# One transformer block on one core: issuing the score products of both head pairs of a slot in one interleaved order, and moving the full-array work between slots

## The chip, the cores and the metric

The kernel runs on 1 core of a Trainium2 chip, in one launch. The metric is the device time of that launch in microseconds (us), lower is better. TensorE (PE) multiplies matrices into PSUM, VectorE (DVE) and ScalarE (ACT) read PSUM, GpSimd (POOL) works on SBUF alone, and SyncE (SP) issues most of the DMA transfers.

## The reference

For 32 sequences of 512 tokens with 256 channels and 16 heads of 16 channels, all in float32:

```python
qk = x @ W_attn + b_attn                  # q and k; v is x itself
y  = causal_attn(q, k, v)                 # softmax(q k^T / 4) v, masked
e  = v[:, :, 1:] - y[:, :, :-1]
k2 = x[:, :-1] @ W_k2 + b_k2
y2 = causal_attn(q[:, :, 1:], k2, e)      # shifted by one, first row zero
x  = layernorm(x + proj(y) + proj(y2))
x  = layernorm(x + ffn(x))                # ffn: 8 experts, top 2
```

The tokens of the experts are those of the first sequence alone; every other sequence gets the two layer norms.

## The kernel before, in words

The 32 sequences have 4 **groups** of 4 heads each, 128 groups in all. `step(n)` works on several groups at once, as a pipeline: it projects for later groups, takes the largest scores of group n, the exponentials of group n-2 and of its second attention n-3, and the weighted values of n-2 and n-3.

A head has 16 channels but sits on 32 partitions, so the four heads of a group lie in the four row **quadrants** of the PE array. **Pair 0** is heads 0 and 1 (quadrants 0 and 1), **pair 1** is heads 2 and 3 (quadrants 2 and 3). Two kinds of work use quadrants:

- `maxima(n, u, pair)`: for one of five units u and one pair it fills a two-bank PSUM tile `sm` with four bf16 mask products (L206, `pick` times `hide`, widths 128, 96, 64, 32 or twice that) and then with the scores of queries with keys (L219); DVE then takes row maxima (L230) into `mx`.
- `scores(n, u, pair)`: it fills a PSUM tile `sc` with scores that lie the other way (L265, keys times `qm`); ACT takes exponentials into `pt` (L274), and POOL zeroes what is above the diagonal (L278).

Each float32 product of one head is two LDWEIGHTS and two MATMUL rows in the trace: two **passes**.

A step has five **slots**. In each slot s PE is given, in this order, `scores` of pair 1, `maxima` of pair 0, `scores` of pair 0, `maxima` of pair 1:

```python
for s in range(len(units)):
    for pair in range(2):
        scores(n - 2, s, 1 - pair)
        if ready(n):
            maxima(n, s, pair)
    for f in rest[s]:
        f()
```

What stands in `rest[s]` follows the slot and needs the whole array: `augment` (4 transposes `mt` of the maxima, L236; DVE adds q to give `qm`, L240), `normalize` (4 transposes `yt`, L304; DVE takes denominators, reciprocals and the scaled values, L308 to L324), `project` (`pj`, L169; ACT adds a bias into the staging tile `pk`, L173, and eight DMAs on SP's queue, L184, spread it over `q_t` or `kk_t`), `values` (`av`, 32 passes in column tiles, L289; ACT copies to `avs`, L297), once in four steps `turn` (`ys`, L355) and two halves of `attended` (`po`, L367, then layer norms on DVE and POOL), and in eight steps the experts (`hidden`, `down`).

PE's order is written out by hand (`manual_schedule`); the other engines are ordered by the tile framework. All PSUM tiles, of slots and of the rest, come from one pool of 4 buffers with two banks each, and the first product into a tile waits until the last reader of the buffer is done. `pk` has two one-buffer tags, `half0` and `half1`, which `hidden` uses too.

The order of a step before, with its full-array parts (which of them a step has depends on n mod 4):

| n mod 4 | order | PE time |
|---|---|---|
| 0 | s0, mt, yt, s1, po, s2, po, s3, av, s4, yt, pj, av | 24.91 us |
| 1 | s0, mt, yt, s1, pj, s2, s3, av, s4, yt, pj, av | 23.18 us |
| 2 | s0, mt, yt, s1, s2, s3, av, s4, yt, pj, av | 21.45 us |
| 3 | s0, mt, yt, s1, pj, s2, ys, s3, av, s4, yt, pj, av | 24.00 us |

Of the kernel before, what the change touches and what calls it, by code (L numbers as in the profile page):

```python
# [1 line left out]

# [6 lines left out]
F32 = mybir.dt.float32  # L9
BF16 = mybir.dt.bfloat16  # L10
I32 = mybir.dt.int32
AF = mybir.ActivationFunctionType
ALU = mybir.AluOpType
AX = mybir.AxisListType

P = 128
HD = 16
HS = 32
GH = 4
NH2 = 2  # L20
# [7 lines left out]
def block_kernel(  # L28
# [16 lines left out]
    nc = tc.nc  # L45
    B, T, C = x.shape
    NB = T // P
    NC = C // P
    NG = C // (GH * HD)
    E = w_gu.shape[0]  # L50
# [5 lines left out]
    const = ctx.enter_context(tc.tile_pool(name="const", bufs=1))  # L56
    seq = ctx.enter_context(tc.tile_pool(name="seq", bufs=2))
    grp = ctx.enter_context(tc.tile_pool(name="grp", bufs=3))
    work = ctx.enter_context(tc.tile_pool(name="work", bufs=2))
# [22 lines left out]
        )  # L82


    q_t = [const.tile([P, T], F32, name=f"q_t{i}") for i in range(4)]
    kk_t = [const.tile([P, 2, T], F32, name=f"kk_t{i}") for i in range(6)]
    wp_sb = const.tile([P, NC, C], F32, name="wp_sb")
    nc.scalar.dma_start(wp_sb, w_proj.rearrange("(c p) f -> p c f", p=P))
# [49 lines left out]
    seqs = {}  # L138
# [26 lines left out]
    def project(two, m):  # L165
        b, half = divmod(two, NG // 2)
        ps = bank2(f"pj{two}_{m}")
        for c in range(NC):
            nc.tensor.matmul(  # L169
                ps[:, 0], wq_sb[:, m, c, half * P : (half + 1) * P], seqs[b]["xT"][:, c], start=(c == 0), stop=(c == NC - 1)  # L170
            )
        pk = work.tile([P, T], F32, tag=f"half{(two + m) % 2}", name=f"pk{two}_{m}", bufs=1)
        nc.scalar.activation(pk, ps[:, 0], AF.Identity, bias=bp_qk[:, m, half : half + 1])  # L173
        for k in range(2):
            n = 2 * two + k
            d = groups.setdefault(n, {})
            if m == 0:
                t = d["q"] = q_t[n % len(q_t)]
            else:
                d["kk"] = kk_t[n % len(kk_t)]  # L180
                t = d["kk"][:, m - 1]
            for h in range(GH):
                r = (GH * k + h) * HD
                nc.sync.dma_start(t[HS * h : HS * h + HD], pk[r : r + HD])  # L184
# [10 lines left out]
    ]  # L195

    def maxima(n, u, pair):
        d = groups[n]
        parts, first, step, kinds = units[u]
        ps = bank2(f"sm{n}_{u}_{pair}")  # L200
        blocks = ps.rearrange("p h (k c) -> p h k c", c=P)
        heads = [(hh, slice(HS * (NH2 * pair + hh), HS * (NH2 * pair + hh + 1))) for hh in range(NH2)]

        for c in range(NB):
            for hh, rows in heads:
                nc.tensor.matmul(  # L206
                    blocks[:, hh, first::step, HS * c :],
                    pick[rows, c],
                    hide[rows, c, kinds[0] : kinds[1], HS * c :],
                    start=(c == 0),  # L210
                    stop=False,
                )
        for i, a, na, at in parts:
            nk = (i + 1) * P
            view = ps[:, :, at * P : at * P + na * nk].rearrange("p h (a k) -> p h a k", k=nk)
            order = [slice(i * P, nk), slice(0, i * P)] if i else [slice(0, P)]
            for keys in order:
                for hh, rows in heads:
                    nc.tensor.matmul(  # L219
                        view[:, hh, :, keys],  # L220
                        d["q"][rows, i * P : (i + 1) * P],
                        d["kk"][rows, a : a + na, keys],
                        start=False,
                        stop=(at == parts[-1][3] and keys == order[-1]),
                    )
        for i, a, na, at in parts:
            nk = (i + 1) * P
            view = ps[:, :, at * P : at * P + na * nk].rearrange("p h (a k) -> p h a k", k=nk)
            to = mx[n % 2][:, i, NH2 * pair : NH2 * (pair + 1), HD + a : HD + a + na]
            nc.vector.tensor_reduce(to, view, AX.X, ALU.max)  # L230

    def augment(n):
        d = groups[n]
        ps = bank2(f"mt{n}")
        for i in range(NB):
            nc.tensor.transpose(  # L236
                ps[:, 0, i * P : (i + 1) * P], mx[n % 2][:, i].rearrange("p h s -> p (h s)"), ident
            )
        d["qm"] = grp.tile([P, T], F32, tag="qm", name=f"qm{n}")
        nc.vector.tensor_add(d["qm"], ps[:, 0], d["q"])  # L240

# [9 lines left out]
    def scores(n, u, pair):  # L253
        parts = [p for p in banks[u] if 0 <= n - p[0] < n_all]
        if not parts:
            return
        ps = bank2(f"sc{n}_{u}_{pair}")
        pt = work.tile([P, NH2, T], F32, tag=f"pt{u}", name=f"pt{n}_{u}_{pair}")
        for a, j, at in parts:
            d = groups[n - a]  # L260
            nq = T - j * P
            d["pt", a, j, pair] = pt[:, :, at * P : at * P + nq]
            for hh in range(NH2):
                rows = slice(HS * (NH2 * pair + hh), HS * (NH2 * pair + hh + 1))
                nc.tensor.matmul(  # L265
                    ps[:, hh, at * P : at * P + nq],
                    d["kk"][rows, a, j * P : (j + 1) * P],
                    d["qm"][rows, j * P :],
                    start=True,
                    stop=True,  # L270
                )
        lo = parts[0][2] * P
        hi = parts[-1][2] * P + T - parts[-1][1] * P
        nc.scalar.activation(pt[:, :, lo:hi], ps[:, :, lo:hi], AF.Exp, scale=HD**-0.5)  # L274

        for a, j, at in parts:
            diag = pt[:, :, at * P : (at + 1) * P]
            nc.gpsimd.affine_select(  # L278
                diag, diag, pattern=[[0, NH2], [1, P]], compare_op=ALU.is_ge, fill=0.0, base=-a, channel_multiplier=-1
            )  # L280

    def values(n, a):
        b, g = divmod(n, NG)
        d = groups[n]
        vals = (v_pad, e_pad)[a]
        ps = bank2(f"av{n}_{a}")
        for j in range(NB):
            for h in range(GH):
                nc.tensor.matmul(  # L289
                    ps[HS * h : HS * (h + 1), 0, j * P :],  # L290
                    vals[:, j, g * GH + h, :],
                    d["pt", a, j, h // NH2][:, h % NH2],
                    start=(j == 0),
                    stop=(j == NB - 1),
                )
        avs = d["avs", a] = work.tile([P, T], F32, tag="avs", name=f"avs{n}_{a}")
        nc.scalar.copy(avs, ps[:, 0])  # L297

    def normalize(n, a):
# [3 lines left out]
        for i in range(NB):  # L303
            nc.tensor.transpose(ps[:, 0, i * P : (i + 1) * P], d["avs", a][:, i * P : (i + 1) * P], ident)  # L304
        got = ps[:, 0].rearrange("p (n h s) -> p n h s", h=GH, s=HS)
        den = small.tile([P, NB, GH], F32, tag="den", name=f"den{n}_{a}")

        nc.vector.tensor_scalar_max(den, got[:, :, :, HD], 1e-30)  # L308
        rden = small.tile([P, NB, GH], F32, tag="rden", name=f"rden{n}_{a}")
        nc.vector.reciprocal(rden, den)  # L310
        rb = rden.unsqueeze(3).to_broadcast([P, NB, GH, HD])
        cols = slice(g * GH * HD, (g + 1) * GH * HD)

# [68 lines left out]
    def twice_normed(b, half):  # L382
# [11 lines left out]
        for k in range(2):  # L394
            i = 2 * half + k
            nc.gpsimd.tensor_scalar(t[:, i], t[:, i], mv[:, k, 0:1], r[:, k : k + 1], ALU.subtract, ALU.mult)  # L396
        if half:
            nc.sync.dma_start(out[b].rearrange("(n p) c -> p n c", p=P), t)
            seqs.pop(b)


    moe = {}
# [90 lines left out]
    def step(n):  # L493
# [7 lines left out]
        if ready(n):  # L501
            prepare(n)
        if ready(n - 1):
            rest[0].append(lambda: augment(n - 1))
        if ready(n - 3):
            rest[0].append(lambda: normalize(n - 3, 0))
            rest[3].append(lambda: values(n - 3, 1))
            rest[4].append(lambda: normalize(n - 3, 1))
        two = n // 2 + 1
        if ready(2 * two):  # L510
            for m, s in [(0, 4)] if n % 2 == 0 else [(1, 1), (2, 4)]:
                rest[s].append(lambda m=m: project(two, m))
        if ready(n - 2):
            rest[4].append(lambda: values(n - 2, 0))
# [2 lines left out]
            rest[2].append(lambda: turn(b))  # L517
        b2, r2 = divmod(n - 5, NG)
        if r2 == NG - 1 and 0 <= b2 < B:
            rest[1].append(lambda: attended(b2, 0))  # L520
            rest[2].append(lambda: attended(b2, 1))
        e = n - first_expert
        if e == -1:
            rest[4] += [route, turn_tokens, lambda: load_expert(0)]
        if 0 <= e < E:
            if e + 1 < E:
                load_expert(e + 1)
            rest[1].append(lambda: hidden(e, 0))
            rest[2].append(lambda: hidden(e, 1))
            rest[4].append(lambda: down(e))  # L530
        if e == E:
            rest[4].append(lambda: second_norm(0, moe["acc"]))
        for s in range(len(units)):
            for pair in range(2):
                scores(n - 2, s, 1 - pair)
                if ready(n):
                    maxima(n, s, pair)
            for f in rest[s]:
                f()

# [1 line left out]
    load_next(0)  # L542
    for m in range(3):
        project(0, m)
    for n in range(max(n_all + 5, first_expert + E + 1)):
        step(n)


# [71 lines left out]
```

## Time and profile before

| | |
|---|---|
| median of 3 runs | 3235.0 us (3234.16 to 3240.43) |
| profiled execution, its own time | 3252.37 us |
| its span in the trace | 3250.7 us |
| PE busy | 3159.7 us (97%) |
| DVE / ACT / POOL busy | 1999.3 / 1668.7 / 1373.8 us |
| mean granted PE clock | 0.986 |
| four steps, n = 18 to 121 | 93.53 us, the same in 26 sequences within 0.01 us |

Busy time of PE is a union over quadrants that work at the same time, with modelled ends: 97% doesn't mean that all four quadrants are in use. The times of slots and parts below are from the first start of a part to the first start of the next in the timeline. A matmul's duration in the trace is longer than its stream[...].

### The profile page before, as it was taken

What the parts mean: (1) busy time and instruction counts of PE and PEld (TensorE: products, weight loads), DVE (VectorE), ACT (ScalarE), POOL (GpSimd) and SP (SyncE); (2) the same over time, 40 slices, a digit from 0 to 9 for tenths busy, and PEclk for the clock granted to TensorE, in tenths of its full rate; (3) what the DMA queues carried; (4) which work ended last, traced back from release to release, by engine and by line L of the source; (5) the groups of instructions that cost most, each with busy time, mean ns of one, the idle gap of its engine ahead of it and who ended that gap; (6) DMA issues with size and microseconds to landing.
All of it is one profiled execution on the core that took longest, in us unless ns stands there. A gap on an engine that the chain in (4) does not pass through costs nothing.

```text
span 3250.7 us, 98094 instructions
## 1 busy us (share of the span) xinstructions
PE 3159.7 (97%) x42312; PEld 2147.1 (66%) x42312; DVE 1999.3 (62%) x3120; ACT 1668.7 (51%) x1823; POOL 1373.8 (42%) x2847
## 2 busy tenths in 40 slices
PE   5999998999999999999999999999999999999997
PEld 4665555667666666666666666676767676676673
DVE  4664444566666666666666666666666666666662
ACT  2554344455555555555555555555555555555554
POOL 4333334344444344444444444444344444443444
PEclk8999999999999999999999999999999999999998
DMA  4111111111111111111111111111111111111110
GB/s 110 37 28 47 37 48 35 39 50 51 32 50 51 41 51 50 50 46 39 50 44 47 50 50 50 39 44 50 40 51 51 49 51 33 50 48 43 38 28 20
DMA packets 144241, 148.13 MB, mean 46 GB/s; under 512 B 40984, under 2 KB 108992, under 8 KB 143808
## 3 DMA queue, kind: packets, MB, share of 16 engines
q1 hardware_dynamic: 143296, 141.42, 16.0%
q8 instruction: 333, 5.46, 0.7%
q14 instruction: 100, 0.82, 0.1%
q10 hardware_dynamic: 416, 0.39, 0.0%
q0 software_dynamic: 96, 0.04, 0.0%
HBM read 74.63 MB, written 16.78 MB: 28 GB/s over the span
## 4 chain that ended last, share of the span: by engine, by line
PE 88%; POOL 5%; DVE 2%; ACT 2%; issue 1%; SPq 1%; DMA 1%; POOLq 0%; DVEq 0%; ACTq 0%
PE sm L219 28%; PE av L289 18%; PE sc L265 14%; PE pj L169 10%; PE sm L206 5%; PE yt L304 4%; POOL h L396 2%; PE mt L236 2%; PE po L367 2%; POOL pt L278 1%; PE gu L450 1%; PE ys L355 1%; PE dn L473 1%; ACT pt L274 1%; POOL r L393 1%
## 5 line engine op out<-in xcount | busy, mean ns | idle before, releaser
L230 DVE TENSOR_REDUCE mx<-sm 128x2 f32<-128x1024 f32 (+3 forms) x1792 | 1573.6, 916 | 965.2 <-PE sm L219 933.0
L274 ACT ACTIVATE pt<-sc 128x1024 f32<-128x1024 f32 (+1 forms) x1282 | 1297.3, 1023 | 683.7 <-PE sc L265 633.6
L219 PE MATMUL sm<-kk_t,q_t 32*128 32x128 f32 (+2 forms) x12288 | 1431.4, 360 | 13.2 <-DMA kk_t<-pk 13.2
L265 PE MATMUL sc<-qm,kk_t 32*128 32x256 f32 (+3 forms) x8192 | 1369.1, 444 | 1.4 <-DVE mx L230 1.2
L278 POOL TENSOR_SCALAR_AFFINE_SELECT pt<-pt 128x256 f32<-128x256 f32 x2048 | 793.1, 408 | 1256.2 <-ACT pt L274 1255.2
L219 PEld LDWEIGHTS sm<-kk_t,q_t 32*128 32x128 f32 x12288 | 920.7, 188 | 35.4 <-issue 8.5
L265 PEld LDWEIGHTS sc<-qm,kk_t 32*128 32x128 f32 x8192 | 711.1, 185 | 224.9 <-issue 134.6
L206 PE MATMUL sm<-hide,pick 32*128 32x128 bf16 (+5 forms) x10240 | 512.3, 217 | 3.8 <-ACT pt L274 3.4
L206 PEld LDWEIGHTS <-pick 32*128 32x128 bf16 x10240 | 368.8, 93 | 32.0 <-issue 12.3
L169 PE MATMUL pj<-xT,wq_sb 128*128 128x512 f32 x768 | 369.7, 604 | 19.8 <-DMA xT<-in_xT 19.8
L297 ACT COPY avs<-av 128x512 f32<-128x512 f32 x256 | 150.1, 586 | 453.3 <-PE av L289 453.3
L289 PE MATMUL av<-pt,e_pad 128*32 128x512 f32 (+3 forms) x4096 | 315.4, 449 | 24.3 <-ACT pt L274 17.2
L289 PE MATMUL av<-pt,v_pad 128*32 128x512 f32 (+3 forms) x4096 | 303.9, 437 | 4.8 <-POOL pt L278 4.8
L173 ACT ACTIVATE pk<-pj,bp_qk 128x512 f32<-128x512 f32 x192 | 132.0, 688 | 337.2 <-PE pj L169 316.4
L289 PEld LDWEIGHTS av<-pt,e_pad 128*32 128x32 f32 x4096 | 134.2, 112 | 243.2 <-issue 139.8
L289 PEld LDWEIGHTS av<-pt,v_pad 128*32 128x32 f32 x4096 | 120.0, 110 | 248.9 <-issue 115.0
L169 PEld LDWEIGHTS pj<-xT,wq_sb 128*128 128x128 f32 x768 | 131.5, 191 | 121.7 <-issue 93.9
L304 PE MATMUL yt<-ident,avs 128*128 128x128 f32 x1024 | 161.4, 280 | 3.8 <-DVE mx L230 2.9
L321 POOL TENSOR_TENSOR e_pad<-xs,y 128x256 f32<-128x256 f32 x128 | 93.4, 730 | 151.2 <-DVE y L320 151.1
L396 POOL TENSOR_SCALAR h<-h,mv,r 128x256 f32<-128x256 f32 x124 | 150.8, 1223 | 6.5
L367 PE MATMUL po<-wp_sb,ysT 128*128 128x256 f32 x512 | 131.4, 401 | 5.7 <-ACT pt L274 4.6
L325 POOL TENSOR_TENSOR y<-y,y 128x256 f32<-128x256 f32 x128 | 93.9, 734 | 90.6 <-DVE y L324 90.6
(76 smaller groups left out, 1405.5 us busy)
## 6 DMA issues: line engine op xcount, KB each, us to landing
kk_t<-pk SPq DMA_DIRECT2D x1024, 32.0 KB
xT<-in_xT SPq DMA_DIRECT2D x32, 512.0 KB
x<-in_x SPq DMA_DIRECT2D x32, 512.0 KB
q_t<-pk SPq DMA_DIRECT2D x512, 32.0 KB
xr<-in_x SPq DMA_DIRECT2D x32, 512.0 KB
out<-h SPq DMA_DIRECT2D x31, 512.0 KB
xs<-in_x SPq DMA_DIRECT2D x32, 384.0 KB
gu<-in_w_gu SPq DMA_DIRECT2D x8, 512.0 KB
```

What stands on the lines that cost most here:

```text
L169: nc.tensor.matmul(ps[:, 0], wq_sb[:, m, c, half * P : (half + 1) * P], seqs[b]["xT"][:, c], start=(c == 0), stop=(c == NC - 1))
L206: nc.tensor.matmul(blocks[:, hh, first::step, HS * c :], pick[rows, c], hide[rows, c, kinds[0] : kinds[1], HS * c :], start=(c == 0), stop ...
L219: nc.tensor.matmul(view[:, hh, :, keys], d["q"][rows, i * P : (i + 1) * P], d["kk"][rows, a : a + na, keys], start=False, stop=(at == part ...
L230: nc.vector.tensor_reduce(to, view, AX.X, ALU.max)
L265: nc.tensor.matmul(ps[:, hh, at * P : at * P + nq], d["kk"][rows, a, j * P : (j + 1) * P], d["qm"][rows, j * P :], start=True, stop=True,)
L274: nc.scalar.activation(pt[:, :, lo:hi], ps[:, :, lo:hi], AF.Exp, scale=HD**-0.5)
L278: nc.gpsimd.affine_select(diag, diag, pattern=[[0, NH2], [1, P]], compare_op=ALU.is_ge, fill=0.0, base=-a, channel_multiplier=-1)
L289: nc.tensor.matmul(ps[HS * h : HS * (h + 1), 0, j * P :], vals[:, j, g * GH + h, :], d["pt", a, j, h // NH2][:, h % NH2], start=(j == 0), ...
L297: nc.scalar.copy(avs, ps[:, 0])
L304: nc.tensor.transpose(ps[:, 0, i * P : (i + 1) * P], d["avs", a][:, i * P : (i + 1) * P], ident)
L367: nc.tensor.matmul(ps[:, 0, i * C : (i + 1) * C], s["ysT"][:, c, (2 * half + i) * P : (2 * half + i + 1) * P], wp_sb[:, c], start=(c == 0) ...
L396: nc.gpsimd.tensor_scalar(t[:, i], t[:, i], mv[:, k, 0:1], r[:, k : k + 1], ALU.subtract, ALU.mult)
```

## The change

Products of a slot are no longer issued as they are made. `maxima` and `scores` return a list of (cost, function) and a function that issues what follows on DVE, ACT and POOL; the new `slot` gives each pair its own stream (pair 0: `maxima`, then `scores`; pair 1: `scores`, then `maxima`), computes when each product would start if the pair's quadrants did nothing else, and issues all products sorted by the start of the **product before it** in its stream. The four masks come in the order 128, 32, 64, 96 instead of 128, 96, 64, 32.

The rest moves: `augment` from slot 0 to slot 3; the first `normalize` from slot 0 to slot 1; `project` from slot 4 to slot 1 (m=0) and slot 2 (m=2); the first `attended` and the first `hidden` from slot 1 to slot 0. Thus most steps have nothing between slots 0 and 1. The store of a result is issued one step later, in slot 1. `augment` adds q in two instructions, a copy on ACT and a sum on POOL, instead of one on DVE. `normalize` of the first attention drops the clamp of the denominator. `values` takes its key blocks in the order 0, 2, 1, 3 (first attention) and 0, 1, 3, 2 (second). There are 5 tiles `q_t` instead of 4, and the tag of `pk` is computed from `two * 3 + m` instead of `two + m`.

```diff
-        pk = work.tile([P, T], F32, tag=f"half{(two + m) % 2}", name=f"pk{two}_{m}", bufs=1)
+        pk = work.tile([P, T], F32, tag=f"half{(two * 3 + m) % 2}", name=f"pk{two}_{m}", bufs=1)
...
-        for c in range(NB):
-            for hh, rows in heads:
-                nc.tensor.matmul(
...
+        for c in (0, *range(NB - 1, 0, -1)):
+            work.append(((kinds[1] - kinds[0]) * (P - HS * c), partial(mask, c)))
...
+                work.append((4 * na * (keys.stop - keys.start), partial(score, view, i, a, na, keys, stop)))
+
+        def largest():
+            for view, to in views:
+                nc.vector.tensor_reduce(to, view, AX.X, ALU.max)
+
+        return work, largest
...
-        nc.vector.tensor_add(d["qm"], ps[:, 0], d["q"])
+        nc.scalar.copy(d["qm"], ps[:, 0])
+        nc.gpsimd.tensor_add(d["qm"], d["qm"], d["q"])
...
+    def slot(n, u):
+        streams = []
+        for pair in range(2):
+            sc = partial(scores, n - 2, u, pair)
+            mm = partial(maxima, n, u, pair) if 0 <= n < n_all else lambda: ([], lambda: None)
+            streams.append([mm, sc] if pair == 0 else [sc, mm])
+        todo = []
+        second = [(1, 0), (0, 0), (0, 1), (1, 1)]
+        started, done = [-1, -1], [0, 0]
+        for pair, k in second:
+            products, after = streams[pair][k]()
+            for m, (cost, emit) in enumerate(products):
+                last = m == len(products) - 1
+                todo.append((started[pair], len(todo), pair, emit, after if last else None))
+                started[pair], done[pair] = done[pair], done[pair] + cost
+        for _, _, pair, emit, after in sorted(todo, key=lambda t: t[:2]):
+            for hh in range(NH2):
+                h = NH2 * pair + hh
+                emit(hh, slice(HS * h, HS * (h + 1)))
+            if after:
+                after()
...
-        for j in range(NB):
+        order = [0, 2, 1, 3] if a == 0 else [0, 1, 3, 2]
+        for j in order:
...
-        nc.vector.tensor_scalar_max(den, got[:, :, :, HD], 1e-30)
+        if a:
+            den = small.tile([P, NB, GH], F32, tag="den", name=f"den{n}")
+            nc.vector.tensor_scalar_max(den, sums, 1e-30)
...
-            rest[0].append(lambda: augment(n - 1))
+            rest[3].append(lambda: augment(n - 1))
         if ready(n - 3):
-            rest[0].append(lambda: normalize(n - 3, 0))
+            rest[1].append(lambda: normalize(n - 3, 0))
...
-            for m, s in [(0, 4)] if n % 2 == 0 else [(1, 1), (2, 4)]:
+            for m, s in [(0, 1)] if n % 2 == 0 else [(1, 1), (2, 2)]:
...
-            rest[1].append(lambda: attended(b2, 0))
+            rest[0].append(lambda: attended(b2, 0))
...
+            rest[1].append(lambda: store(b3))
...
-            rest[1].append(lambda: hidden(e, 0))
+            rest[0].append(lambda: hidden(e, 0))
...
-            for pair in range(2):
-                scores(n - 2, s, 1 - pair)
-                if ready(n):
-                    maxima(n, s, pair)
+            slot(n, s)
```

## The prediction

> **What bounds the kernel now.** First the shares of busy time and the chain that ended last, from the page.
>
> ```profile
> PE 3159.7 (97%) x42312; PEld 2147.1 (66%) x42312; DVE 1999.3 (62%) x3120; ACT 1668.7 (51%) x1823; POOL 1373.8 (42%) x2847
> ...
> PE 88%; POOL 5%; DVE 2%; ACT 2%; issue 1%; SPq 1%; DMA 1%; POOLq 0%; DVEq 0%; ACTq 0%
> ```
>
> PE carries the time. But 97% is a union over four quadrants, so the question is how full they are. PE's timeline of one slot 0 tells:
>
> ```profile
> 1501.72 0.48 PE L265 MATMUL sc<-qm,kk_t 32*128 32x256 f32 x2
> 1501.75 0.32 PE L206 MATMUL sm<-hide,pick 32*128 32x128 bf16 x8
> ...
> 1502.26 0.60 PE L265 MATMUL sc<-qm,kk_t 32*128 32x256 f32 x4
> 1502.55 0.48 PE L219 MATMUL sm<-kk_t,q_t 32*128 32x384 f32 x2
> 1502.87 0.38 PE L265 MATMUL sc<-qm,kk_t 32*128 32x256 f32 x2
> 1502.89 0.32 PE L206 MATMUL sm<-hide,pick 32*128 32x128 bf16 x8
> ```
>
> Pair 1's last `sc` pass starts at 1502.48 and streams 0.21 us, so its quadrants are free at 1502.69. Its masks start only at 1502.89, just after pair 0's `sc` began at 1502.87. Before that, pair 0's quadrants had four later passes issued and waiting (two products of two). In slot 3, with only two such passes waiting, pair 1 was not held (masks at 1515.67, where its `sc` ended). I read: about four passes of one quadrant can stand issued, and a fifth blocks everything behind it, whatever its quadrant. Slots 0, 2 and 4 lose 0.2 to 0.3 us to this.
>
> Slot 1 loses more, to something else:
>
> ```profile
> 1503.08 2.36 DVE L230 TENSOR_REDUCE mx<-sm 128x2 f32<-128x1024 f32 x2 [3.62 <-PE sm L219]
> 1505.36 0.68 DVE L240 TENSOR_TENSOR qm<-mt,q_t 128x512 f32<-128x512 f32 x1
> 1505.49 0.37 PE L206 MATMUL sm<-hide,pick 32*128 32x256 bf16 x4
> 1506.44 0.42 DVE L320 TENSOR_TENSOR y<-yt,rden 128x256 f32<-128x256 f32 x1
> 1506.92 0.42 PE L206 MATMUL sm<-hide,pick 32*128 32x256 bf16 x6
> ```
>
> Pair 0's masks (1505.49) wait for the second reduction of slot 0, which ended at 1505.44, pair 1's (1506.92) for the PSUM tile of `yt`, which DVE released at 1506.86; its quadrants were free at 1506.08. The short gap `mt`, `yt` (1.02 us) put DVE's work in the way. Slots standing alone take 2.37, 3.14, 2.60, 2.40 and 2.63 us to the next part; without a pause between them slots 2 and 3 take 5.21, slots 1 to 3 8.54.
>
> Last, what a semaphore wait does to matmuls behind it, from the timeline near the end:
>
> ```profile
> 3215.17 1.07 PE L289 MATMUL av<-pt,v_pad 128*32 128x512 f32 x8
> ...
> 3215.84 1.68 POOL L278 TENSOR_SCALAR_AFFINE_SELECT pt<-pt 128x256 f32<-128x256 f32 x4 [2.01 <-ACT pt L274]
> 3217.22 1.50 PE L289 MATMUL av<-pt,v_pad 128*32 128x384 f32 x24 [0.98 <-POOL pt L278]
> ```
>
> The second key block waits for POOL until 3217.22. The third (256 wide, 3217.89) had its data long before and still came after it. So a waiting product holds all later ones.
>
> **What the skill says.** The Trainium skill, "Perfetto Trace Analysis", section "Tensor Engine Instruction (MATMUL, LD_WEIGHTS)", has PE's instructions wait for semaphores in a queue and then move to an execution FIFO with limited reorder; the 3217 lines agree with the first part. "TensorE: Matmul & The Clock Gate", section "The mechanism", says that matmuls keep program order and only LDWEIGHTS is pulled ahead. The trace differs: masks issued after both `sc` products started at 1501.75, before the first product's second pass (1502.04). Across quadrants order isn't kept; the measurement decides.
>
> **The change, part by part.** Times of one profiled execution, sums per four steps (93.54 us before).
>
> *Slots alone.* With each pair free to run, pair 1 of slot 0 takes 0.11 (start) + 0.85 (`sc`, 2048 columns in all passes) + 0.16 (masks) + 0.92 (two products; 0.85 streaming, the rest the first weight load, seen as a first pass of 351 ns instead of 270) = 2.04 us, and 0.1 to drain: 2.14. The new order never puts more than two products (four passes) of a quadrant in the queue, so I let it reach that. Slot 3 likewise 2.14 (now 2.40); slots 1, 2 and 4 have masks twice as wide, 0.28: 2.24, 2.23 and 2.24 (now 3.14, 2.60, 2.63). The new mask order shows at most 0.05 per slot, and it is in these.
>
> *Slots without a pause (joints).* These are slots 0 and 1 in three steps of four, slots 2 and 3 where n mod 4 = 2. By the built program's order and PSUM buffers, a joint's second slot (1 or 3) issues `sc` of pair 1, two masks of pair 0, and then **the first mask of pair 1**, whose buffer is freed by the second exponential of the slot before. Exponentials take 1.02 us; they start 1.26 and 2.31 into slot 0 (1527.89 after a slot that began at 1526.63), so it is free at 3.39. Pair 0's own buffer is free at 2.62 (first reduction 1.34 to 2.57). Hence pair 0 stands from 2.7 to 3.39, behind a wait that isn't its own. Then its masks 0.14, products 0.90, `sc` 0.85: 5.28; pair 1, interleaved, ends at 5.26. With the drain 5.38, against 2.37 + 3.14 now. Slots 2 and 3 joined come to 5.40 by the same working, no better than now.
>
> *Rest.* `mt` before `av` hides behind nothing new, 0.49 as before. `yt` 0.49, `pj` 1.81 (1.91 ahead of a slot), `av` 2.29, `po` 1.92 and `ys` 1.02 keep their time. What is late next: after a joint `pj` waits for the first reduction of slot 1 (0.11); `yt` after slot 4 for an exponential (0.1); where n mod 4 = 0, `pj` stands 0.45 behind the layer norm on DVE, `po` 0.2 and 0.1 behind exponentials, and `av` 0.32 behind DVE; where it is 3, slot 3 is held by the copy of `ysT` (2.50 instead of 2.14).
>
> | n mod 4 | sum after | before |
> |---|---|---|
> | 0 | 2.35+1.92+2.24+0.10+0.49+0.45+1.91+2.23+0.11+1.92+2.14+0.21+0.50+0.32+2.29+2.24+0.11+0.49+2.29 = 24.31 | 24.91 |
> | 1 | 5.38+0.49+0.11+1.91+2.23+0.12+1.91+2.24+0.11+0.50+2.29+2.24+0.10+0.49+2.29 = 22.41 | 23.18 |
> | 2 | 5.38+0.49+0.12+1.91+5.40+0.49+0.05+2.29+2.24+0.10+0.49+2.29 = 21.25 | 21.45 |
> | 3 | 5.38+0.49+0.12+1.91+2.23+0.11+1.81+1.02+2.50+0.50+2.29+2.24+0.10+0.49+2.29 = 23.48 | 24.00 |
>
> Together 91.45: 2.09 us less per four steps.
>
> *Other engines.* DVE loses 128 sums of 680 ns and 128 clamps of 164; ACT gains 128 copies (586, as `avs`), POOL 128 sums (about 1.3 us, as `sig` and `hid` of 128x512). All have idle time (POOL 42% busy); `qm` is needed a step later, after `av`, slot 4, `yt` and `av` (7 us) against 0.6 + 1.3 and POOL's queue of selects (0.41 each). I cost it at nothing; without that cover it would be up to 1.9 per step. The DMAs of `project` keep their count and go out earlier; the result's store no longer stands on SP ahead of them. The tag of `pk` doesn't change: 3·two + m and two + m have the same parity. The fifth `q_t` costs one ACT activation at the start (0.71).
>
> *Sum.* 118 steps without experts are 29.5 times 2.09: 62 us. The end: `values` finds ready blocks while it waits, about -2; the start +0.7. The eight steps with experts (34.8 to 49.9 us each) have their own waits (table loads, `pk` and `hf` sharing tiles, a DVE instruction idle for 4.1 us); nothing before shows the new order, so I take 0 and bound it by 2 us a step, -16 to +16. In all -63: 3252.4 becomes 3189; the median shown lies 17.4 below the profiled execution, so 3172.
>
> **Rivals.** *No holding.* If pair 0 went on past pair 1's waiting mask, joints of slots 0 and 1 would end 0.64 sooner, the other 0.55, as its own buffers are free then: 4.56 instead of 2.09 per four steps, 3100. For it: quadrants do overtake each other. Against: 3217.
>
> *Weights late (slower).* A product now enters the queue only when the one before it starts. If that leaves its first weight load exposed as it is after a mask (351 - 270 = 81 ns), on each of some 20 products of a pair per step rather than on 5, it costs 15 x 0.081 = 1.2 us a step, 4.9 per four, net +2.8: 29.5 times that, 3318. It decides from 35 ns per product on. Against it: within a product the second pass follows with no gap[...].
>
> *DVE and ACT take it back.* In joints the reductions (1.22 us, two a slot) and exponentials set the pace, more than I count; at 0.5 us a joint the gain is gone: 3235.
>
> **How the numbers follow.** The forecast case gets 0.55, no holding 0.2, late weights 0.15, taken back 0.1. The forecast's own range is 3172 with 16 for the experts and 0.05 us for each of 20 slots in four steps (30 us): 3130 to 3215. The range goes down to no holding, 3095, and up to 3225; late weights stay outside. About 0.2%, 6.5 us, can be told from no change. Of the taken-back case half ends faster, half the same: faster 0.8, same 0.05, slower 0.15.
>
> **What would show it.** Right: slots 0, 2 and 4 alone 0.2 to 0.4 shorter; pair 1's masks starting where its `sc` ends; slots 0 and 1 joined at 5.4 with pair 0 standing 0.7 inside slot 1; four steps near 91.5. Wrong: joints near 4.8 (no holding), or first passes of 350 ns on most products (late weights); expert steps longer by over 2 us.

## The result and the profile after

On chips where both kernels ran in turns, the median fell from 3247.3 us (20 runs) to 3234.2 us (20 runs): the ratio is 0.9961, with a 95% interval of 0.9948 to 0.9973. The change makes the kernel faster by 0.4%, and not by the 2% forecast. The profiled execution of the changed kernel has a span of 3233.4 us against 3250.7 before.

The first lines to compare are again the shares of busy time and the shares of the chain that ended last (the chain of work followed back from the last instruction), from the page of the kernel after:

```profile
PE 3057.4 (95%) x42312; PEld 1947.3 (60%) x42312; DVE 1867.3 (58%) x2864; ACT 1734.0 (54%) x1956; POOL 1538.0 (48%) x2975
...
PE 61%; ACT 7%; POOL 7%; DVE 4%; issue 3%; SPq 0%; ACTq 0%; POOLq 0%; DMA 0%; DVEq 0%
```

PE has 102 us less busy time, and the span is only 17 us shorter. PE is busy for less of the time. The shares of the chain add up to 82% here, since it could be followed back only to 573 us; of what it covers PE has three quarters, where it had 88%. What PE saved inside the slots came back as waits. The page's costliest groups name one of them:

```profile
L335 PE MATMUL av<-pt,v_pad 128*32 128x512 f32 (+3 forms) x4096 | 309.5, 437 | 41.6 <-POOL pt L294 40.7
```

The last two numbers are idle time of PE just before these matmuls: 41.6 us, 40.7 of it until POOL had zeroed a tile `pt`. By step, with each step counted from the start of slot 0 (means over 24 sequences):

| n mod 4 | before | forecast | after |
|---|---|---|---|
| 0 | 24.91 | 24.31 | 25.72 |
| 1 | 23.18 | 22.41 | 22.52 |
| 2 | 21.45 | 21.25 | 21.45 |
| 3 | 24.00 | 23.48 | 23.41 |
| sum | 93.53 | 91.45 | 93.10 |

Three of the four steps come out within 0.2 us of the forecast. The step with n mod 4 = 0 is 1.4 us over it and is longer than before. (With n mod 4 = 2 that still means no gain at all, where 0.2 was forecast.) POOL's timeline of the last part of one such step (it starts at 1494.26) shows why. The columns are start, duration, engine, line and operation, and in brackets the idle time before it and what ended it:

```profile
1510.80 2.43 POOL L445 TENSOR_SCALAR h<-h,mv,r 128x256 f32<-128x256 f32 x2
1513.19 0.42 POOL L294 TENSOR_SCALAR_AFFINE_SELECT pt<-pt 128x256 f32<-128x256 f32 x1
1514.26 2.36 POOL L399 TENSOR_TENSOR xr<-xr,bp 128x1024 f32<-128x1024 f32 x1 [0.65 <-DMA xr<-in_x]
1516.56 0.42 POOL L294 TENSOR_SCALAR_AFFINE_SELECT pt<-pt 128x256 f32<-128x256 f32 x1
1516.93 1.30 POOL L253 TENSOR_TENSOR qm<-qm,q_t 128x512 f32<-128x512 f32 x1
1518.17 1.51 POOL L294 TENSOR_SCALAR_AFFINE_SELECT pt<-pt 128x256 f32<-128x256 f32 x4
```

The same stretch in PE's timeline:

```profile
1515.49 0.66 PE L350 MATMUL yt<-ident,avs 128*128 128x128 f32 x4
1517.04 1.50 PE L335 MATMUL av<-pt,v_pad 128*32 128x512 f32 x16 [0.89 <-POOL pt L294]
1519.37 1.07 PE L335 MATMUL av<-pt,v_pad 128*32 128x384 f32 x16 [0.83 <-POOL pt L294]
```

POOL has a second half of a layer norm, the sum `xr<-xr,bp` with a wait for its load, and the new sum `qm` to do, and the six selects that `av` needs stand between and behind them. `av` starts 1.55 us after `yt` instead of the 0.59 of the other steps, and stops once more in the middle, for 0.83. Over all steps with n mod 4 = 0, `av` starts 0.85 to 1.55 after `yt`, 1.17 on average, and takes 3.33 instead of 2.29. Before, the same work of POOL, in a step that starts at 1501.72:

```profile
1518.24 2.43 POOL L396 TENSOR_SCALAR h<-h,mv,r 128x256 f32<-128x256 f32 x2
1520.62 0.41 POOL L278 TENSOR_SCALAR_AFFINE_SELECT pt<-pt 128x256 f32<-128x256 f32 x1
1521.00 2.36 POOL L350 TENSOR_TENSOR xr<-xr,bp 128x1024 f32<-128x1024 f32 x1
1523.31 1.84 POOL L278 TENSOR_SCALAR_AFFINE_SELECT pt<-pt 128x256 f32<-128x256 f32 x5
```

Here the selects follow `xr` at once, without `qm`, and `pj` (1.81 us of PE) stood between `yt` and `av`, which began at 1524.34 without a wait. Counted from the start of the step, POOL's layer norm ends at the same place in both kernels (18.95 and 18.97), but its last select ends at 23.4 before and at 25.4 now.

The wait for the load of `xr` comes from the change too. SP's queue in the same step of the kernel after:

```profile
1504.44 5.80 SPq L185 DMA_DIRECT2D q_t<-pk  x8
1510.33 0.54 SPq L398 DMA_DIRECT2D xr<-in_x  x1
```

The old `xr` was read for the last time by the sum `h<-po,xr`, which ended at 1508.60. The load of the next one stands on SP behind the eight DMAs of `project`, which now run after slot 1, and went out 1.7 us later (1.25 on average over such steps). In the kernel before nothing stood there, and it went out 0.03 us after that sum. In the changed kernel POOL waits 0 to 0.66 us for this load, 0.29 on average, and in each of 26 such steps `av` starts 0.85 to 0.90 us plus that wait after `yt`.

Inside the joints the hold that the forecast described is there. PE's timeline in a joint of slots 0 and 1 that starts at 1542.89:

```profile
1545.59 0.31 PE L208 MATMUL sm<-hide,pick 32*128 32x256 bf16 x4
...
1546.25 0.32 PE L208 MATMUL sm<-hide,pick 32*128 32x256 bf16 x6
1546.41 0.63 PE L221 MATMUL sm<-kk_t,q_t 32*128 32x128 f32 x6
```

Pair 0 starts two masks (four rows, two heads) from 1545.59 on and then nothing until 1546.25, right after ACT's second exponential ended and pair 1's first mask got its buffer; the two exponentials in ACT's timeline end at 1546.20:

```profile
1544.15 2.05 ACT L290 ACTIVATE pt<-sc 128x1024 f32<-128x1024 f32 x2 [0.48 <-PE sc L275]
```

The joint takes 5.28 us.

### The profile page after: what moved, and what is told of

Its sections match the earlier page's. It is cut to its first block, busy times and chain, and to the rows that moved or that the text cites. A ratio compares the mean times of both kernels' runs of the same rounds, so it can differ in the third digit from the quotient of the medians.

```text
span 3233.4 us, 97999 instructions
## 1 busy us (share of the span) xinstructions
PE 3057.4 (95%) x42312; PEld 1947.3 (60%) x42312; DVE 1867.3 (58%) x2864; ACT 1734.0 (54%) x1956; POOL 1538.0 (48%) x2975
## 4 chain that ended last, share of the span: by engine, by line
PE 61%; ACT 7%; POOL 7%; DVE 4%; issue 3%; SPq 0%; ACTq 0%; POOLq 0%; DMA 0%; DVEq 0%
PE sm L221 13%; PE av L335 13%; PE sc L275 12%; PE pj L170 10%; ACT pt L290 7%; PE po L416 4%; PE yt L350 3%; PE sm L208 3%; POOL h L445 2%; POOL pt L294 2%; PE mt L248 2%; DVE st L438 1%; DVE h L423 1%; POOL qm L253 1%; DVE mx L240 1%
## 5 line engine op out<-in xcount | busy, mean ns | idle before, releaser
L240 DVE TENSOR_REDUCE mx<-sm 128x2 f32<-128x1024 f32 (+3 forms) x1792 | 1541.1, 914 | 1092.1 <-PE sm L221 1083.0
L275 PE MATMUL sc<-qm,kk_t 32*128 32x256 f32 (+3 forms) x8192 | 1384.3, 448 | 26.2 <-ACT pt L290 7.8
L221 PE MATMUL sm<-kk_t,q_t 32*128 32x128 f32 (+2 forms) x12288 | 1286.0, 351 | 12.8 <-DMA kk_t<-pk 12.8
L221 PEld LDWEIGHTS sm<-kk_t,q_t 32*128 32x128 f32 x12288 | 909.7, 187 | 29.3 <-DMA kk_t<-pk 13.6
L208 PE MATMUL sm<-hide,pick 32*128 32x128 bf16 (+5 forms) x10240 | 541.1, 216 | 8.5 <-DVE mx L240 7.8
L170 PE MATMUL pj<-xT,wq_sb 128*128 128x512 f32 x768 | 386.2, 627 | 29.5 <-DMA xT<-in_xT 19.5
L208 PEld LDWEIGHTS <-pick 32*128 32x128 bf16 x10240 | 351.4, 92 | 84.2 <-issue 67.4
L335 PE MATMUL av<-pt,v_pad 128*32 128x512 f32 (+3 forms) x4096 | 309.5, 437 | 41.6 <-POOL pt L294 40.7
L335 PEld LDWEIGHTS av<-pt,e_pad 128*32 128x32 f32 x4096 | 124.3, 111 | 160.8 <-issue 126.3
L253 POOL TENSOR_TENSOR qm<-qm,q_t 128x512 f32<-128x512 f32 x128 | 163.9, 1281 | 16.9 <-ACT qm L252 9.6
L350 PEld LDWEIGHTS yt<-ident,avs 128*128 128x128 f32 x1024 | 108.5, 142 | 65.9 <-ACT pt L290 50.5
```

Of the source, the lines that this page charges most:

```text
L170: nc.tensor.matmul(ps[:, 0], wq_sb[:, m, c, half * P : (half + 1) * P], seqs[b]["xT"][:, c], start=(c == 0), stop=(c == NC - 1))
L208: nc.tensor.matmul(blocks[:, hh, first::step, HS * c :], pick[rows, c], hide[rows, c, kinds[0] : kinds[1], HS * c :], start=(c == 0), stop ...
L221: nc.tensor.matmul(view[:, hh, :, keys], d["q"][rows, i * P : (i + 1) * P], d["kk"][rows, a : a + na, keys], start=False, stop=stop,)
L253: nc.gpsimd.tensor_add(d["qm"], d["qm"], d["q"])
L275: nc.tensor.matmul(ps[:, hh, at * P : at * P + T - j * P], d["kk"][rows, a, j * P : (j + 1) * P], d["qm"][rows, j * P :], start=True, stop ...
L335: nc.tensor.matmul(ps[HS * h : HS * (h + 1), 0, j * P :], vals[:, j, g * GH + h, :], d["pt", a, j, h // NH2][:, h % NH2], start=(j == orde ...
```

## The experiments

The theory: the parts on PE went nearly as forecast, and POOL's queue at the end of steps with n mod 4 = 0 took back three quarters of the gain. Three parts of the change meet there: `qm` summed on POOL, `project` moved out of slot 4, and slots that end earlier. The rivals: the hold in joints is the whole loss; or the merged order gives nothing at all and the moves are what counts.

**qm back to one DVE sum.**

```diff
-        nc.scalar.copy(d["qm"], ps[:, 0])
-        nc.gpsimd.tensor_add(d["qm"], d["qm"], d["q"])
+        nc.vector.tensor_add(d["qm"], ps[:, 0], d["q"])
```

> The changed kernel with one part undone: qm is again one DVE sum from PSUM, so POOL has no qm sum (1.28 us each). Theory POOL: in the step with n mod 4 = 0 POOL works without a break for 10 us (layer norm, xr, selects, qm), and values waits 1.04 us inside for the selects behind qm; that wait goes, four steps drop from 93.1 to about 92.1, the whole by some 31 us (1.3 to 1.4% below the kernel before, which the changed kernel is by 0.4%). The 0 to 1 us that yt and the start of av lose in this step stays, since it stands behind xr and not behind qm. Theory PE order: the gain was lost in the slots; then nothing moves by more than 0.2%.

Measured: 3209.4 us, 0.9888 of before (0.9872 to 0.9904); four steps 92.2. `av` never waits inside any more: it takes 2.29 us, and the step with n mod 4 = 0 falls to 24.8. A wait ahead of `av` remains in these steps, with `yt` to `av` 0.85 to 1.90: the sum `xr` and the wait for its load are still in front of the selects. The theory holds, with a part left over; the whole is 1.1% below before, where 1.3 to 1.4% was expected.

**The sum xr moved to DVE.**

```diff
-        nc.gpsimd.tensor_add(s["xr"], s["xr"], bp2.unsqueeze(1).to_broadcast([P, NB, C]))
+        nc.vector.tensor_add(s["xr"], s["xr"], bp2.unsqueeze(1).to_broadcast([P, NB, C]))
```

> The changed kernel with the sum of xr and the bias (2.36 us once in four steps) on DVE instead of POOL; qm stays on ACT and POOL. Theory POOL: both waits of the step with n mod 4 = 0 go (about 0.6 us on average ahead of av, 1.04 us inside), less up to 0.3 for DVE's extra work: four steps 91.5 to 91.8, the whole 1.7 to 1.9% below the kernel before. Theory PE order: within 0.2% of the changed kernel.

Measured: 3302.4 us, 1.0183 of before (1.0159 to 1.0206). A miss, and an instructive one. DVE's timeline:

```profile
1541.68 1.95 DVE L399 TENSOR_TENSOR xr<-xr,bp 128x1024 f32<-128x1024 f32 x1 [3.60 <-DMA xr<-in_x]
1543.55 2.41 DVE L240 TENSOR_REDUCE mx<-sm 128x2 f32<-128x1024 f32 x3
```

The load of `xr` goes out when the sum `h<-po,xr` has read the old tile and SP's queue is past the DMAs of `project`, and the framework puts the sum of `xr` early in DVE's order. DVE stands 3.60 us for the load, and the reductions that release PSUM stand behind it; over the whole run it is 96.9 us in 31 such waits. POOL also stood for this load, for 0.65 us, because other work kept it busy until then. The Trainium skill, "Perfetto Trace Analysis", section "Tensor Engine Instruction (MATMUL, LD_WEIGHTS)", calls DVE, ACT and GpSimd strictly first in, first out; these lines agree. Slot 4 of these steps takes 5.42 us on average instead of 2.34. Moving the sum was no test of the theory, since it added a wait of its own, so the sum was left out instead.

**The sum xr left out.** The kernel then lacks the bias of the projection in its result.

```diff
-        nc.gpsimd.tensor_add(s["xr"], s["xr"], bp2.unsqueeze(1).to_broadcast([P, NB, C]))
```

> After, with POOL's sum xr<-xr,bp left out (the output lacks the bias of the projection). Theory (POOL's queue in the last part of steps n mod 4 = 0 is what av waits for; the sum takes 2.36 and 0.65 of waiting for its load there): three us less in that queue, the waits of yt and av gone, the step at 24.3 as forecast, 29 times 1.4 = 41 us less than after: 0.983 to 0.985 of before. Rival (av waits for ACT's exponentials, and POOL only shows as the last in line): 0.993 or more.

Measured: 3180.8 us, 0.9803 of before (0.9781 to 0.9824), a little more gain than expected. The step with n mod 4 = 0 takes 24.10 us and four steps 91.5; the forecast had 24.31 and 91.45. POOL's timeline at the same place, then PE's:

```profile
1502.90 0.77 POOL L294 TENSOR_SCALAR_AFFINE_SELECT pt<-pt 128x256 f32<-128x256 f32 x2
1503.65 1.27 POOL L253 TENSOR_TENSOR qm<-qm,q_t 128x512 f32<-128x512 f32 x1
1505.23 0.77 POOL L294 TENSOR_SCALAR_AFFINE_SELECT pt<-pt 128x256 f32<-128x256 f32 x2 [0.32 <-ACT pt L290]
```

```profile
1505.21 0.66 PE L350 MATMUL yt<-ident,avs 128*128 128x128 f32 x4
1505.80 2.36 PE L335 MATMUL av<-pt,v_pad 128*32 128x512 f32 x32
```

POOL is now early enough to wait for ACT (0.32), and `av` follows `yt` in 0.59 and runs through. The rival, that `av` waits for ACT and POOL only shows as the last in line, is refuted. `qm` is still on POOL and costs nothing there: with `xr` out of the way the forecast's "nothing" would have been right.

**project of m=0 back in slot 4, in steps with n mod 4 = 0.**

```diff
-            for m, s in [(0, 1)] if n % 2 == 0 else [(1, 1), (2, 2)]:
+            for m, s in [(0, 4 if n % 4 == 0 else 1)] if n % 2 == 0 else [(1, 1), (2, 2)]:
```

> After, with the projection m=0 of steps n mod 4 = 0 back behind yt in slot 4, where it stood before. Theory (av waits for POOL there because pj, 1.8 us, no longer stands between slot 4 and av): the wait of av (1.0 inside, 0.96 ahead) goes; against it slot 2 now follows yt without pj and waits about 0.2 for DVE and ACT; the step falls from 25.7 to about 24.5, 29 times 1.2 = 35 us less than after: 0.985 of before. Rival (POOL is so late there that 1.8 us of cover don't reach; or slot 2 loses as much as av gains): within 0.3% of after, 0.993 to 0.999.

Measured: 3204.5 us, 0.9871 of before (0.9851 to 0.9892); the step takes 24.69 us in nearly all sequences, four steps 92.0. `pj` covers POOL's queue and the wait of `av` is gone, 1.7 us of it. The rival has its share: slot 2, now right behind `yt`, takes 3.00 instead of 2.34 us, where 0.2 more was expected. The edit also takes the eight DMAs away from in front of the load of `xr`, for which POOL now waits 0.05 us on average instead of 0.29; how much that alone is worth was not tried.

**Pair 1's first mask later in joints.** In slots 1 and 3 the first mask of pair 1 gets a later place in the sort (700 in the sort's own units of cost), behind pair 0's masks and first products:

```diff
-                todo.append((started[pair], len(todo), pair, emit, after if last else None))
+                key = max(started[pair], 700) if (pair, k, m) == (1, 1, 0) and done[pair] > 700 else started[pair]
+                todo.append((key, len(todo), pair, emit, after if last else None))
```

> The changed kernel with one key raised: where pair 1 has a one-part sc (slots 1 and 3), its first mask is issued after pair 0's first two products instead of after pair 0's second mask. Theory holding: pair 0 no longer stands about 0.6 us behind a wait that is pair 1's; slots 0 and 1 joined drop from 5.28 to about 4.8, slots 2 and 3 joined from 5.35 to about 4.8; four steps 2 us less unless DVE is late, the whole 2.2 to 2.4% below the kernel before. Theory no holding (the 0.55 us gap between pair 0's masks has another cause, such as DVE or the quadrant's queue): joints stay within 0.1 us.

Measured: 3176.0 us, 0.9783 of before (0.9765 to 0.9801); joints 4.90 (slots 0 and 1) and 4.97 (2 and 3) instead of 5.28 and 5.35, where about 4.8 was expected; four steps 91.2. PE's timeline in a joint that starts at 1543.61:

```profile
1546.21 0.45 PE L208 MATMUL sm<-hide,pick 32*128 32x256 bf16 x8
...
1546.49 0.65 PE L221 MATMUL sm<-kk_t,q_t 32*128 32x128 f32 x6
```

All four masks of pair 0 (eight rows) come at once and its products at 1546.49, 2.88 into the joint, where they stood until 3.5 in the joint above. The hold is real, and it is the order alone that makes it. But the step with n mod 4 = 0 stays at 25.8: the hold is a second, separate loss. The forecast had included it, so it is no part of the miss.

**The merged order alone, on the kernel before.** `slot` and the new mask order, all else as before.

> The kernel before with the interleaved issue order of the slots alone (with the new order of masks); everything between slots stays where it was, qm on DVE, 4 q_t tiles. Theory POOL: without the moves and the qm sum nothing is given back in the step with n mod 4 = 0: slots 4 and 2 drop to 2.34 (from 2.63 and 2.60), slot 3 to 2.31 (from 2.40), slot 1 by about 0.2, slot 0 stays near 2.35 as mt waits for the first exponential; joints of slots 1 to 3 stay; four steps 91 to 91.5, the whole about 2% below before. Theory PE order: the merged order itself costs what it gains, and four steps stay at 93.1 to 93.5 or more.

Measured: 3231.1 us, 0.9954 of before (0.9938 to 0.997); four steps 92.7, where 91 to 91.5 was expected. Slots 0, 2 and 4 alone fall to 2.34, as expected, and slot 1 from 3.14 to 3.06, but slots 2 and 3 joined go from 5.21 to 5.33, and slots 1 to 3 joined from 8.54 to 9.11. `av` in the step with n mod 4 = 0 takes 2.40 instead of 2.29, so POOL can have taken back 0.1 at most here.

**The same with the late mask.** The edit of the late mask on top of the merged order alone.

> The kernel before with the merged order alone, and pair 1's first mask late where its scores come in one part. The merged order alone gave 0.9954, four steps 92.70; slots 2 and 3 joined took 5.33, slots 1 to 3 joined 9.12. Theory (what merging gives to single slots it loses in joints to pair 1's first mask): 0.38 less in each of the two joints with a slot 3, as much again where slot 1 opens the long joint: four steps 91.6 to 92.0, 0.984 to 0.988 of before. Rival (with the gaps of before the reductions or exponentials set the pace of the joints): no change, 0.995.

Measured: 3190.7 us, 0.9831 of before (0.981 to 0.9853); joints 4.97 and 8.39, four steps 91.6. What merging gave to single slots, the hold had taken back in the joints. The joints are as expected, and the time is just below the range that was expected.

**The moves alone.** The changed kernel with each slot's products stream by stream and the masks in the old order.

```diff
-        for c in (0, *range(NB - 1, 0, -1)):
+        for c in range(NB):
...
-        for _, _, pair, emit, after in sorted(todo, key=lambda t: t[:2]):
+        for _, _, pair, emit, after in todo:
```

> After, with the products of a slot issued stream by stream and the masks in the old order, as before; all moves between slots stay. Theory (merging is worth 0.2 to 0.3 us in each slot that stands alone, and costs 0.1 to 0.3 in a joint, since pair 0 stands behind pair 1's first mask there): slots alone go back to 2.60 (s2), 2.63 (s4), 2.40 (s3), joints of s0 and s1 shrink from 5.28 to about 5.0, s2 and s3 from 5.35 to 5.21; per four steps +2.5 for slots alone, -1.0 for joints, so about +1.5 of 93.1: 1.008 to 1.014 of before. Rival (the interleaved order does nothing that the moves don't): the same as after, 0.996.

Measured: 3235.7 us, 0.9972 of before (0.9958 to 0.9987). A miss by 1%: the slots are as expected (2.60, 2.63, 2.31; joints 5.11 and 5.21), yet the time is nearly that of the changed kernel. Summing all parts between 450 and 3000 us of the two traces gives the balance of merging on top of the moves: single slots 55.8 us less, joints 16.9 more, from the start of `yt` to the next part 26.4 more, `pj`, `mt` and `av` together 8.5 more. In the 26.4 it isn't `yt` that waits, but what stands behind it. After joints it is `pj`, for the first reduction of slot 1. DVE, then PE, in the changed kernel:

```profile
1547.53 1.29 DVE L240 TENSOR_REDUCE mx<-sm 128x2 f32<-128x768 f32 x2 [0.86 <-PE sm L221]
```

```profile
1548.27 0.65 PE L350 MATMUL yt<-ident,avs 128*128 128x128 f32 x4
1548.96 1.10 PE L170 MATMUL pj<-xT,wq_sb 128*128 128x512 f32 x2
```

The reduction (two instructions) ends at 1548.82, and `pj` starts 0.70 us after `yt`; with the moves alone it is 0.49. In three steps of four that makes some 16 us. Most of the rest is `av` in steps with n mod 4 = 0, which starts 1.17 after `yt` instead of 0.80: slot 4 ends 0.3 sooner, and POOL does not.

The run shows one thing more. With the old, longer slots `av` stops inside for as long as in the changed kernel (3.32 us in all), and the step with n mod 4 = 0 takes 26.0. So POOL's loss comes with the moves and the sum `qm`; that slots end earlier adds only to the wait ahead of `av`. And of the rival "the merged order gives nothing and the moves are what counts" the first half is true only with the hold in joints: alone the merged order gives 0.5% with the hold and 1.7% without it, the moves 0.3%.

**The two edits together.** `qm` on DVE and the late mask.

> The two edits that gained, together: qm summed on DVE in one instruction, and pair 1's first mask late in joints. Theory (one frees POOL ahead of av in steps n mod 4 = 0, the other takes the hold out of joints; different places): the gains add, 0.73% and 1.78% below after, about 0.971 of before, four steps at 90.1. Rival (the same slack is counted twice: shorter joints bring POOL's selects closer together, and av waits for them again): no better than the late mask alone, 0.978.

Measured: 3151.3 us, 0.9698 of before (0.9675 to 0.972); four steps 90.2. They add up.

**With the projection back in slot 4 as well.**

> The two edits that gained (qm in one DVE sum; pair 1's first mask late) and m=0's projection of steps n mod 4 = 0 back in slot 4. Without the last, 0.9698, and one stretch of four steps varies from 24.4 to 25.4 us because av and yt still wait for POOL behind the sum xr. Theory (pj covers what is left of that wait): the stretch steady at about 24.5, 0.4 less per four steps: 0.966. Rival (slot 2 right behind yt gives the same back to DVE and ACT): 0.969 to 0.972.

Measured: 3146.4 us, 0.9697 of before (0.9675 to 0.9719); the step steady at 24.70, four steps 89.9. No gain that can be told from none: what `av` gains slot 2 gives back, as the rival had it.

**The bias on DVE behind the residual sum.** Besides the two edits, POOL's sum is left out and DVE adds the bias itself:

```diff
-        nc.gpsimd.tensor_add(s["xr"], s["xr"], bp2.unsqueeze(1).to_broadcast([P, NB, C]))
...
+        nc.vector.tensor_add(s["h"][:, two], s["h"][:, two], bp2.unsqueeze(1).to_broadcast([P, 2, C]))
```

> The two edits that gained, and the sum xr<-xr,bp of POOL (2.36 us and its wait for the load) replaced by two sums of bp on DVE right after h<-po,xr, 128x512 each in SBUF, at most 0.69 as that row. Theory (POOL's queue there is what is left of the wait): the stretch falls from 24.4 to 25.4 to about 23.7, less up to 0.5 for the two DVE sums ahead of the layer norm and of slot reductions: 0.4 to 1.0 per four steps, 0.959 to 0.966. Rival (DVE's sums delay pj and the reductions by as much as POOL's sum cost): 0.970 to 0.974.

Measured: 3176.7 us, 0.979 of before (0.9766 to 0.9814): a loss against the two edits alone, and worse than the rival had it. The step with n mod 4 = 0 rises from 24.9 to 25.6, four steps take 90.9. DVE's timeline, then PE's:

```profile
1483.78 0.69 DVE L422 TENSOR_TENSOR h<-po,xr 128x512 f32<-128x512 f32 x1 [0.62 <-PE po L415]
1484.50 0.69 DVE L425 TENSOR_TENSOR h<-h,bp 128x512 f32<-128x512 f32 x1
...
1486.12 2.45 DVE L240 TENSOR_REDUCE mx<-sm 128x2 f32<-128x768 f32 x4
```

```profile
1487.52 1.96 PE L170 MATMUL pj<-xT,wq_sb 128*128 128x512 f32 x4 [0.89 <-DVE mx L240]
...
1497.46 2.36 PE L335 MATMUL av<-pt,e_pad 128*32 128x512 f32 x32 [0.82 <-DVE mx L240]
```

Each sum of 0.69 delays the slot's reductions, and `pj` and the other `av` wait for the buffer that those free. DVE has 37% of idle time in this kernel, but not here.

**The sum xr later on POOL.** Besides the two edits, one more reader of the tile `xr` behind the second `normalize` of the step, a DVE product of 128x16; the next load can start only after it:

```diff
+            if g == 1 and b >= 1:
+                hold = small.tile([P, NB, GH], F32, tag="hold", name=f"hold{n}")
+                nc.vector.tensor_mul(hold, seqs[b - 1]["xr"][:, :, 0:GH], rden)
```

> The two edits that gained (qm in one DVE sum; pair 1's first mask late), and one more reader of the tile xr: a DVE product of 128x16 behind the second normalize of steps n mod 4 = 0, so that the next load of xr starts only there and POOL's sum xr<-xr,bp falls into the next step, behind the copy to v_pad. Theory (the sum costs nothing by itself, only where it stands: ahead of the selects that av waits for): the step n mod 4 = 0 at 24.1, as with the sum left out, four steps at 89.4, 0.7 less than with the two edits alone: 0.962 to 0.965 of before. Rival (in the next step the sum, waiting about 5 us for its load, holds the selects of slots 0 and 1 and with them av): 0.970 or more.

Measured: 3128.2 us, 0.9645 of before (0.9622 to 0.9668), the fastest version. The step takes 24.10 us, four steps 89.4, both as expected. POOL's timeline around the end of such a step:

```profile
1480.39 0.77 POOL L293 TENSOR_SCALAR_AFFINE_SELECT pt<-pt 128x256 f32<-128x256 f32 x2 [0.26 <-ACT pt L289]
1481.89 0.73 POOL L374 TENSOR_TENSOR y<-y,y 128x256 f32<-128x256 f32 x1 [0.73 <-DVE hold L377]
...
1485.72 2.36 POOL L402 TENSOR_TENSOR xr<-xr,bp 128x1024 f32<-128x1024 f32 x1 [2.76 <-DMA xr<-in_x]
1488.03 2.21 POOL L293 TENSOR_SCALAR_AFFINE_SELECT pt<-pt 128x256 f32<-128x256 f32 x6
```

POOL now stands 2.76 us for the load and sums for 2.36 at the start of the next step, with six selects behind, and the step isn't longer for it (21.98): no `av` is near. The sum costs by its place, not by its length.

All together (four steps: mean over the sequences of one trace, experts left out; ratio to before):

| kernel | four steps, us | ratio |
|---|---|---|
| before | 93.5 | 1 |
| after | 93.1 | 0.9961 |
| merged order alone | 92.7 | 0.9954 |
| merged order alone, late mask | 91.6 | 0.9831 |
| moves alone | 93.2 | 0.9972 |
| after, late mask | 91.2 | 0.9783 |
| after, qm on DVE | 92.2 | 0.9888 |
| after, xr on DVE | 95.3 | 1.0183 |
| after, projection in slot 4 | 92.0 | 0.9871 |
| after, without the sum xr | 91.5 | 0.9803 |
| after, qm on DVE, late mask | 90.2 | 0.9698 |
| the same, projection in slot 4 | 89.9 | 0.9697 |
| the same, bias on DVE | 90.9 | 0.979 |
| the same, xr later | 89.4 | 0.9645 |

"The same" is the kernel with `qm` on DVE and the late mask, each time with one more edit.

## Why the prediction was wrong

*The sign* was right, the size was not: 13 us instead of 63.

*The step that failed* is "Other engines", where the POOL sum of `qm` and the earlier DMAs of `project` are costed at nothing. The forecast compared when `qm` is needed (7 us later) with the time of `qm` itself and named POOL's queue of selects only as a delay of `qm`. It did not ask what is queued on POOL behind `qm`: the selects of slots 3 and 4, which `av` of the same step needs. It left out the other things that POOL does at that place, the layer norm's second half and the sum `xr`, of 2.36 us. It moved `pj` out of slot 4 without counting that `pj` was the cover of those selects. And it did not ask which load stands on SP behind the eight DMAs that now go out earlier.

The step with n mod 4 = 0 pays 1.62 us for this (25.72 against 24.10 without `xr`): `av` stands 1.04 inside, and starts 0.58 late, of which 0.29 is POOL's wait for the load. In some 29 such steps it is 47 us, against a miss of 50. That `qm`, the moved `pj` and `xr` are needed together is shown: undoing any one of them takes more than half of the 1.62 away (`qm` on DVE 0.9, `pj` back in slot 4 1.0, `xr` left out all of it). The bound of the forecast, "up to 1.9 per step", has nearly the size of the 1.62, but by coincidence: it is the time of `qm` itself, and what waits is `av`, for selects. Nothing of it was carried into the range, which stopped at 3225.

*The parts on PE* were right in the main. Slots alone, with the waits that the sums have, were forecast at 2.34 to 2.35 and took 2.31 to 2.34; only the one ahead of which `ysT` is copied was forecast at 2.50 and took 2.33. Joints were forecast at 5.38 and 5.40 and took 5.28 to 5.36. Without the sum `xr`, four steps take 91.5 against 91.45, and the ratio 0.9803 is that of the forecast (3189 to 3252.4: 0.9805). A part of this agreement is luck: n mod 4 = 0 was forecast 0.2 too long, 1 and 2 too short by 0.1 and 0.2; in the steps with n mod 4 = 1 and 3 the joint came out 0.1 shorter and the wait of `pj` behind it 0.1 longer (0.21 where 0.11 was forecast). The forecast also names two sizes for one thing. Its sum for n mod 4 = 1 takes slot 3 at 2.24, where its text has 2.14; and among its signs slot 0 alone was to be 0.2 to 0.4 shorter, while its own sum has it at 2.35 against 2.37, and it took 2.34. That about four passes of one quadrant can stand issued, its reading of why slots were slow before, was tried by no run of its own; pair 1's masks now start where its `sc` ends, as they should by that reading.

*The mechanism of joints* was right: pair 0 stands behind pair 1's first mask, and the late mask frees it. The rival "no holding" is thereby refuted for the change as it is, and nearly describes the edited kernel: it gave joints of 4.74 and 4.85, and they take 4.90 and 4.97.

*Weights late* did not happen: single slots would have stayed as long as before or grown, and by the merged order alone they fell by 0.03 (slot 0) to 0.29 (slot 4).

*DVE and ACT take it back*, given 0.1, was in part true, but after the slots and not in the joints. `pj` behind a joint waits 0.1 longer for DVE than forecast. `yt` waits for exponentials 129 times in the changed kernel, 32 us in all, and 8 us with the moves alone; the forecast had counted 0.1 for such a wait, and they have 0.25 on average, a few long ones among them.

*The experts' steps*, costed at nothing within 16 us: from the last `av` of step 9 to that of step 18 PE's timeline has 387.7 us before and 385.2 after, well inside the bound.

## What to carry to other kernels

When work is added to an engine with idle time, the question isn't when its result is needed but what stands behind it in that engine's order, and which of these PE waits for; look for the one stage in which the queue is full, since the average (POOL at 42%) hides it. When a part is moved, list what ran under it: its place may have been the cover for another engine. List what its DMAs will stand in front of, too: here a load waited behind eight of them. And a long instruction that is needed much later can be the whole cost merely by where a scheduler puts it; holding its input back by one more reader was worth as much as leaving the work out.

## What the runs showed of the hardware

- A matmul that waited for a semaphore held the matmuls behind it, those for other quadrants too (pair 0 standing from 1545.7 to 1546.25 for pair 1's buffer); moving one mask back in the order is worth 0.38 us per joint.
- A DVE instruction that waited for a DMA held DVE: 3.60 us in one place, 97 us in the whole run.
- Eight DMAs of `project` took 5.80 us to issue on SP's queue, and the load of `xr` behind them went out 1.7 us after its tile was free; POOL's wait for it (0 to 0.66) moved the start of `av` by as much, within 0.05.
- In the trace of before, passes of one quadrant follow each other by 429 to 432 ns for 512 columns, 323 to 325 for 384, 215 to 219 for 256 and 109 to 110 for 128, while their rows show 587, 481, 374 and 270 ns.
- A sum of 128x512 in float32 took 0.68 to 0.70 us on DVE, with its inputs in SBUF (0.697) or one of them in PSUM (0.692), and 1.28 on POOL. DVE's sum of 128x1024 within SBUF took between 1.21 and 2.27 us; what made it vary was not tried.
